# One wait more in each turn: GpSimd's subtraction behind VectorE's max of the same turn

## The chip, the cores and the metric

The kernel runs on one core of a Trainium2 chip. The metric is the device time of one execution in microseconds (us). The engines are TensorE (PE; its weight loads are shown apart as PEld), VectorE (DVE), ScalarE (ACT), GpSimd (POOL) and SyncE (SP), which only issues transfers here. All five run on their own and meet by semaphores. [...]

## The reference, cut to what matters

Two layers work on eight images x of 256 channels and 32 x 32 places. The change lies in the first, an attention with a learned position bias. For each image and each of four heads, 1024 queries look at 64 sampled keys. The bias of a query and a key is a small network of two inputs, the signed logarithms of the distances in x and in y:

```python
bias = jnp.sign(pos) * jnp.log1p(jnp.abs(pos))
bias = jax.nn.relu(bias @ cpb_w1.T + cpb_b1)      # first layer, 64 hidden channels
bias = jax.nn.relu(bias @ cpb_w2.T + cpb_b2)      # second layer, 64 x 64
bias = bias @ cpb_w3.T + cpb_b3                   # third layer, one value
attn = jax.nn.softmax(sim + bias, axis=-1)
```

It is computed for every pair of query and key: 8 x 4 x 1024 x 64 pairs. The second layer of the kernel is a sigmoid attention over the 1024 tokens of an image, followed by a mixture of eight experts of which each token takes two.

## The kernel before, in words

**Steps and turns.** The bias network is cut into steps. One step holds 128 partitions (two keys times 64 hidden channels) by 1024 elements (two heads, 16 rows and 32 columns of queries). An image has 128 steps (STEPS), taken two at a time in 64 turns (TURNS), so the main loop has 8 x 64 = 512 turns. The step with the even number n and the one with the odd number go different ways.

**First layer.** The network's first layer separates into a term of the column (`ta`) and a negated term of the row (`nb`), prepared once for 16 steps by `terms` (its `scale` is L439 on ScalarE and L440 on VectorE, its `second` is L446 on TensorE and L451 on ScalarE). An even step is a subtraction ta - nb on GpSimd (L465), followed by a ReLU in place on ScalarE (`rectify`, L470). An odd step is a single max(ta, nb) on VectorE (L463), which differs from the ReLU of the difference by nb; that term is put back later through `nc_`. Both read two SBUF tensors and write one `h1` tile of 128 x 1024, of which there are six buffers.

**Second layer.** `second_layer` runs four groups of matmuls on TensorE (L478) for each step into a PSUM tile `h2p`, of which there are two: one for the even and one for the odd step of a turn. The even one is emptied by ScalarE with a ReLU (L484), the odd one by VectorE with a max against `nc_` (L486). So the second layer of one turn needs L484 and L486 of the turn before.

**Third layer and the rest.** `third_layer` adds the product with the third weights into the PSUM tile `sim` (L505) every other turn. Beside this chain, each turn carries a piece of other work, paced by generators: the preparation of the next image (`prep`: the powers L260, the depthwise convolution L286, the sampling weights L368), `softmax` (L537), the sigmoid attention (`attention`: matmuls L713 and L727, sigmoid L718, normalising L579, L580 and L587, the residual sum L680, scatters L775) and the experts with their sums (`experts` L921, L926, L939 and L947; `combine` L984 and the gathers L992).

**Order.** In turn n the loop calls, in this order: the first layer of turn n + 2 (`first_layer`, even and then odd), the second layer of turn n, the ReLU of the new even step, the third layer where it is due, and the other work. `in_order` fixes each engine's queue in the order in which the code issues. On VectorE this gives max of n + 2, L486 of n, other work of n; on ScalarE L484 of n, L470 of n + 2, other work of n; on GpSimd the subtraction of n + 2 and then other work of n. Between engines only semaphores count, so GpSimd may run ahead of VectorE as far as the six buffers let it.

Of the kernel before, what the change touches and what calls it, by code (L numbers as in the profile page):

```python
# [9 lines left out]
F32 = mybir.dt.float32  # L10
I32 = mybir.dt.int32
AF = mybir.ActivationFunctionType
ALU = mybir.AluOpType
# [3 lines left out]
P = 128  # L17
# [53 lines left out]
def second_form(b, table, n):  # L71

    return n % 2 == 1
# [30 lines left out]
def tile_conv_attn_hybrid(ctx: ExitStack, tc: tile.TileContext, x, par, qw, w1, w2_, cst, out):  # L104
    nc = tc.nc
# [7 lines left out]
    hpool = ctx.enter_context(tc.tile_pool(name="h", bufs=1))  # L113
# [9 lines left out]
    def big(name):  # L123
        return t8.tile([P, 2, N], F32, tag="t8", name=name)
# [19 lines left out]
    def xin(b):  # L144
        return x[b].rearrange("(k p) h w -> p k (h w)", p=P)
# [278 lines left out]
    def terms(b, k, h, part):  # L424
        number = 4 * k + 2 * h + part
        fd = sts[b]["fd"].rearrange("k (s r) f -> k r s f", r=2)
        ta = abpool.tile([P, 16, 2, 32], F32, name="ta")
        nb = abpool.tile([P, 16, 2, 16], F32, name="nb")
        nc_ = abpool.tile([P, 2, 8, 16], F32, name="nc")
        taf = ta.rearrange("p s g x -> p s (g x)")  # L430
        nbf = nb.rearrange("p s g y -> p s (g y)")
        ss = slice(part * 16, (part + 1) * 16)
        for r in range(2):
            rs = slice(64 * r, 64 * r + 64)
            nc.sync.dma_start(out=taf[rs], in_=fd[k, r, ss, 0:64].partition_broadcast(64))
            nc.sync.dma_start(out=nbf[rs], in_=fd[k, r, ss, 64 + 32 * h : 96 + 32 * h].partition_broadcast(64))

        def scale():
            nc.scalar.activation(taf, taf, AF.Identity, bias=par_("cb1"), scale=par_("w1x"))  # L439
            nc.vector.tensor_scalar(nbf, nbf, par_("w1y"), -1.0, ALU.mult, ALU.mult)  # L440

        def second():
            cps = [psum("cp") for _ in range(2)]
            for r, g in ((0, 0), (1, 1), (0, 1), (1, 0)):
                rs, gs = slice(64 * r, 64 * r + 64), slice(64 * g, 64 * g + 64)
                nc.tensor.matmul(  # L446
                    cps[r][gs, 0:128], lhsT=par_("w2")[rs, gs], rhs=nb[rs, 1::2, g, :],
                    start=True, stop=True, tile_position=(64 * r, 64 * g),
                )
            for r in range(2):  # L450
                nc.scalar.activation(  # L451
                    nc_[:, r].rearrange("p s y -> p (s y)"), cps[r][:, 0:128], AF.Identity, bias=ncb2,
                )

        return (ta, nb, nc_, b, number), scale, second

    def first_layer(terms_, n):
        ta, nb, nc_, of, number = terms_
        h1 = hpool.tile([P, 2, 16, W], F32, name="h1", bufs=6)
        a = ta[:, n].unsqueeze(2).to_broadcast([P, 2, 16, W])  # L460
        b = nb[:, n].unsqueeze(3).to_broadcast([P, 2, 16, W])
        if second_form(of, number, n):
            nc.vector.tensor_tensor(h1, a, b, ALU.max)  # L463
            return h1, nc_[:, :, n // 2]
        nc.gpsimd.tensor_tensor(h1, a, b, ALU.subtract)  # L465
        return h1, None

    def rectify(h1, nc_):
        if nc_ is None:
            nc.scalar.activation(h1, h1, AF.Relu)  # L470
# [3 lines left out]
    def second_layer(h1, nc_):  # L474
        h2p = ps_h.tile([P, 2, 512], F32, tag="h2p", name="h2p")
        for r, g in ((0, 0), (1, 1), (0, 1), (1, 0)):
            rs, gs = slice(64 * r, 64 * r + 64), slice(64 * g, 64 * g + 64)
            nc.tensor.matmul(  # L478
                h2p[gs, r, :], lhsT=par_("w2")[rs, gs], rhs=h1[rs, g].rearrange("p y x -> p (y x)"),
                start=True, stop=True, tile_position=(64 * r, 64 * g),  # L480
            )
        h2 = hpool.tile([P, 2, 512], F32, name="h2", bufs=6)
        if nc_ is None:
            nc.scalar.activation(h2, h2p, AF.Relu, bias=par_("cb2"))  # L484
            return h2
        nc.vector.tensor_tensor(  # L486
            h2.rearrange("p r (y x) -> p r y x", x=W), h2p.rearrange("p r (y x) -> p r y x", x=W),
            nc_.unsqueeze(3).to_broadcast([P, 2, 16, W]), ALU.max,
        )
        return h2  # L490
# [507 lines left out]
    class Side:  # L998
# [5 lines left out]
        def step(self):  # L1004
            busy = False
            if self.waiting and not (sorting and self.busy):
                busy = self.busy
                self.busy = next(self.waiting[0], None)
                if self.busy is None:
                    self.waiting.pop(0)  # L1010
                    self.busy = True
            if self.left and not busy and not sorting:
                self.left = next(self.prep, self) is not self
# [10 lines left out]
    table, scale, second = terms(0, 0, 0, 0)  # L1024
    while "sampled" not in sts[0]:
        next(first)
    scale()
    second()
    h1s = [first_layer(table, n) for n in range(4)]
    for h in h1s:  # L1030
        rectify(*h)
    run(first)
# [4 lines left out]
    def place(t):  # L1037
        b, s = divmod(t, STEPS)
        return b, s // 64, s // 32 % 2

    def logits(t):
        b, k, h = place(t)
        ss = third_layer(sts[b], k, h, t // 4 % 8, h2s[:4])
        del h2s[:4]
        if ss is None:
            return None
        if (k, h) == (0, 0):
            os_[b] = big("o")
        if (k, h) == (1, 1):
            sts[b]["last"] = ss  # L1050
        else:
            return softmax(sts[b], k, h, ss, os_[b], aside)

    def residual(b):
        xres[b] = big("x")
        nc.sync.dma_start(out=xres[b], in_=xin(b))

    def advance(what):
        for steps in list(what):
            if next(steps[1], what) is what:  # L1060
                what.remove(steps)
# [3 lines left out]
    def mix(b, i):  # L1065
        of = mixtures[0][0] if mixtures else NB
        if of == b - 2 and b < NB - 1:
            due = i in (24, 26) or i > 26 and i % 2 and i not in (35, 37, 39, 59, 61, 63)
        elif of == b - 3:
            due = i == 9  # L1070
        else:
            due = b == NB - 1 and (i >= TURNS - 2 if of == b - 1 else of < b and i > 9 and (i % 2 or i % 3 == 0))
        if due:
            step(mixtures)
# [5 lines left out]
    for n in range(NB * TURNS):  # L1080
        b, i = divmod(n, TURNS)
        if i == 0:
            steps = iter(())
            if b + 1 < NB:
                xb = big("xb")
                nc.sync.dma_start(out=xb, in_=xin(b + 1))
                steps = prep(b + 1, xb, sts[b + 1])
            side = Side(steps)
        if b == 0 and i in (8, 16):
            nc.sync.dma_start(  # L1090
                out=xss[i // 8 - 1].rearrange("(t p) c -> p t c", p=P),
                in_=zero.unsqueeze(1).to_broadcast([P, ROWS // P, C]),
            )
        if i == 46:
            residual(b)
        coming_ = (n // 8 + 1) * 16
        if coming_ < total and n % 8 == 0:
            b_, k_, h_ = place(coming_)
            coming, scale, second = terms(b_, k_, h_, coming_ // 16 % 2)
        if n % 8 == 6 and coming_ < total:  # L1100
            table = coming
        new = []
        if n + 2 < NB * TURNS:
            new = [first_layer(table, (2 * n + 4 + r) % 16) for r in range(2)]
        h1s += new
        h2s += [second_layer(*h1s.pop(0)) for _ in range(2)]
        for h in new:
            rectify(*h)
        ready = n % 2 == 0 and n and logits(2 * n - 1)
        if coming_ < total:  # L1110
            if n % 8 == 3:
                scale()
            elif n % 8 == 4:
                second()
        if i > 4:
            side.step()
        if ready:
            side.waiting.append(ready)
        if i == 0 and b:
            mains.append((b, below))  # L1120
        elif i == 53:
            above, below = attention(b, sts[b], os_.pop(b), {})
            mains.append((b, above))
        advance(mains)
        mix(b, i)
        step(sums)
        if i == TURNS - 1:
            side.finish()
    logits(total - 1)
    mains.append((b, below))  # L1130
    n = sorted_ = 0
# [119 lines left out]
```

## Time and profile before

| What | us |
|---|---|
| median of 3 runs | 3145.4 (3139.6 to 3148.86) |
| profiled execution | 3125.55 |
| its span, first to last instruction | 3123.8 |
| TensorE busy | 2832.1 (91%) |
| VectorE busy | 2170.5 (69%) |
| ScalarE busy | 1824.4 (58%) |
| GpSimd busy | 1558.2 (50%) |

The granted TensorE clock was 0.975 on average. A busy share is an average over stages: the first 200 us hold the start-up, where TensorE is busy for 131 us, and the last 274 us, after the 512 turns, hold the last image's attention and experts, where it is busy for 218 us. In a line of the profile, "L465 POOL" is line 465 of the kernel on GpSimd; the tiles follow as output<-inputs, then partitions x elements. In a line of waits come the total in us, the number of times and the longest.

### The profile page before, as it was taken

What the parts mean: (1) busy time and instruction counts of PE and PEld (TensorE: products, weight loads), DVE (VectorE), ACT (ScalarE), POOL (GpSimd) and SP (SyncE); (2) the same over time, 40 slices, a digit from 0 to 9 for tenths busy, and PEclk for the clock granted to TensorE, in tenths of its full rate; (3) what the DMA queues carried; (4) which work ended last, traced back from release to release, by engine and by line L of the source; (5) the groups of instructions that cost most, each with busy time, mean ns of one, the idle gap of its engine ahead of it and who ended that gap; (6) DMA issues with size and microseconds to landing.
All of it is one profiled execution on the core that took longest, in us unless ns stands there. A gap on an engine that the chain in (4) does not pass through costs nothing. (4 is left out here: it accounts for less than half of the span.)

```text
span 3123.8 us, 51635 instructions
## 1 busy us (share of the span) xinstructions
PE 2832.1 (91%) x19592; PEld 1395.6 (45%) x19592; DVE 2170.5 (69%) x2999; ACT 1824.4 (58%) x2533; POOL 1558.2 (50%) x945
## 2 busy tenths in 40 slices
PE   3888998899999999999999999899999999979975
PEld 2223343233545344453545445354444545514764
DVE  4897678967776687857876678766877574595122
ACT  3666565665576566665566656665666666554322
POOL 2546454744455364645556455553646443383122
PEclk7999999999999999999999999999999999989998
DMA  3312101211256125531346223561245325631386
GB/s 106 83 32 48 21 14 32 58 38 21 75 139 187 23 63 140 168 107 43 77 111 208 51 57 100 144 179 33 61 132 173 88 78 153 173 97 57 112 280 221
DMA packets 428297, 311.21 MB, mean 100 GB/s; under 512 B 284432, under 2 KB 368656, under 8 KB 428048
## 3 DMA queue, kind: packets, MB, share of 16 engines
q1 hardware_dynamic: 415472, 273.14, 32.7%
q0 software_dynamic: 12288, 33.57, 3.4%
q8 instruction: 154, 2.52, 0.3%
q10 hardware_dynamic: 288, 1.20, 0.1%
q14 instruction: 95, 0.78, 0.1%
HBM read 239.93 MB, written 67.90 MB: 99 GB/s over the span
## 5 line engine op out<-in xcount | busy, mean ns | idle before, releaser
L465 POOL TENSOR_TENSOR h<-ta,nb 128x1024 f32<-128x1024 f32 x512 | 1071.6, 2095 | 1036.2 <-PE h2p L478 913.1
L478 PE MATMUL h2p<-h,pr__100 64*64 64x512 f32 x8192 | 1028.3, 610 | 131.8 <-DVE h L486 107.5
L486 DVE TENSOR_TENSOR h<-h2p,nc 128x1024 f32<-128x1024 f32 x512 | 624.6, 1220 | 461.4 <-PE h2p L478 454.7
L484 ACT ACTIVATE h<-h2p,pr__100 128x1024 f32<-128x1024 f32 x512 | 570.9, 1115 | 517.0 <-PE h2p L478 515.8
L463 DVE TENSOR_TENSOR h<-ta,nb 128x1024 f32<-128x1024 f32 x512 | 769.2, 1503 | 0.3
L470 ACT ACTIVATE h<-h 128x1024 f32<-128x1024 f32 x512 | 538.0, 1051 | 63.4 <-POOL h L465 63.2
L478 PEld LDWEIGHTS h2p<-h,pr__100 64*64 64x64 f32 x8192 | 253.7, 133 | 658.0 <-issue 295.1
L505 PE MATMUL sim<-h,pr__100 128*32 128x512 f32 x4096 | 511.5, 618 | 0.0
L505 PEld LDWEIGHTS sim<-h,pr__100 128*32 128x32 f32 x4096 | 109.5, 112 | 377.8 <-issue 377.8
L713 PE MATMUL ap<-qt,tn 128*128 128x256 f32 x1024 | 250.5, 388 | 0.5 <-ACT nc L451 0.5
L727 PE MATMUL vp<-tt,sg 128*128 128x256 f32 x1024 | 243.3, 381 | 0.3 <-ACT sg L718 0.3
L992 POOL DMA_INDIRECT gs<-ys,slot x128 | 139.0, 1086 | 175.3 <-DMA ys<-yt 55.7
L713 PEld LDWEIGHTS ap<-qt,tn 128*128 128x128 f32 x1024 | 185.2, 190 | 88.5 <-issue 55.0
L947 ACT ACTIVATE ht<-hp,w 128x128 f32<-128x128 f32 (+1 forms) x366 | 108.6, 377 | 196.8 <-PE hp L939 173.2
L921 PE MATMUL yp<-w,ht 128*128 128x256 f32 x792 | 196.2, 390 | 13.7 <-DMA w<-in_w 7.0
L727 PEld LDWEIGHTS vp<-tt,sg 128*128 128x128 f32 x1024 | 193.2, 190 | 33.2 <-issue 6.9
L939 PE MATMUL hp<-xg,w 128*128 128x128 f32 (+1 forms) x1464 | 197.0, 287 | 6.7 <-ACT gk L307 2.8
L939 PEld LDWEIGHTS hp<-xg,w 128*128 128x128 f32 x1464 | 187.8, 194 | 18.3 <-ACT gk L307 3.7
L775 POOL DMA_INDIRECT xs<-ut,slot x128 | 167.8, 1311 | 51.0 <-DVE slot L869 29.4
L921 PEld LDWEIGHTS yp<-w,ht 128*128 128x128 f32 x792 | 144.4, 191 | 73.0 <-issue 34.0
L926 DVE TENSOR_TENSOR yt<-yp,w 128x512 f32<-128x512 f32 x99 | 68.3, 690 | 153.5 <-PE yp L921 127.3
L286 DVE SCALAR_TENSOR_TENSOR oc<-qp,pr__100,oc 128x128 f32<-128x128 f32 x280 | 168.9, 603 | 7.2
(266 smaller groups left out, 2468.0 us busy)
## 6 DMA issues: line engine op xcount, KB each, us to landing
w<-in_w SPq DMA_DIRECT2D x183, 384.0 KB, 3.6
w<-in_w SPq DMA_DIRECT2D x183, 257.0 KB, 3.7
ta<-fd SPq DMA_DIRECT2D x128, 256.0 KB, 5.5
xl<-xs SPq DMA_DIRECT2D x99, 256.0 KB, 3.7
ys<-yt SPq DMA_DIRECT2D x99, 256.0 KB, 2.3
nb<-fd SPq DMA_DIRECT2D x128, 128.0 KB, 5.3
xb<-in_x SPq DMA_DIRECT2D x8, 1024.0 KB, 7.2
x<-in_x SPq DMA_DIRECT2D x8, 1024.0 KB
```

What stands on the lines that cost most here:

```text
L286: nc.vector.scalar_tensor_tensor(oc, tap, dw[:, t : t + 1], oc, ALU.mult, ALU.add)
L463: nc.vector.tensor_tensor(h1, a, b, ALU.max)
L465: nc.gpsimd.tensor_tensor(h1, a, b, ALU.subtract)
L470: nc.scalar.activation(h1, h1, AF.Relu)
L478: nc.tensor.matmul(h2p[gs, r, :], lhsT=par_("w2")[rs, gs], rhs=h1[rs, g].rearrange("p y x -> p (y x)"), start=True, stop=True, tile_positi ...
L484: nc.scalar.activation(h2, h2p, AF.Relu, bias=par_("cb2"))
L486: nc.vector.tensor_tensor(h2.rearrange("p r (y x) -> p r y x", x=W), h2p.rearrange("p r (y x) -> p r y x", x=W), nc_.unsqueeze(3).to_broad ...
L505: nc.tensor.matmul(sim[32 * q : 32 * q + 32, :], lhsT=par_("z3")[:, 15 - m : 47 - m], rhs=h2s[2 * u + q // 2][:, q % 2, :], start=False, s ...
L713: nc.tensor.matmul(ap[:, u, :], lhsT=tn[:, k, m0 : m0 + P], rhs=qt[:, k, quarter(q)], start=(k == 0), stop=(k == 1),)
L727: nc.tensor.matmul(vp[:, i, :], lhsT=sg_[:, u, i * P : (i + 1) * P], rhs=tt[:, 2 * mp + u, :], start=(first and u == 0 and i == 0), stop=( ...
L921: nc.tensor.matmul(yp[:, s, :], lhsT=ht[:, f, s * P : (s + 1) * P], rhs=f2[:, s * several // 2, f * C : (f + 1) * C], start=(f == 0), stop ...
L939: nc.tensor.matmul(hp[:, f, us], lhsT=f1[:, u, k * C + f * P : k * C + (f + 1) * P], rhs=xg[:, k, us], start=(k == 0), stop=(k == 1),)
```

## The change

A new function `first_layers` takes both steps of a turn. It takes the two `h1` buffers first, then issues the odd step's max and after it the even step's subtraction, and adds a dependency, carried by a semaphore, of the subtraction on the max. `first_layer` is given its buffer and returns its instruction as a third value. The four steps ahead of the loop are made by two calls. The values computed are the same.

```diff
-    def first_layer(terms_, n):
+    def first_layers(terms_, n):
+        h1s = [hpool.tile([P, 2, 16, W], F32, name="h1", bufs=6) for _ in range(2)]
+        out = [first_layer(terms_, n + r, h1s[r]) for r in (1, 0)]
+        tc.add_manual_dep(
+            out[1][2].ins, out[0][2].ins.name,
+            mybir.DependencyInfo(mybir.DependencyClass.Sync, mybir.DependencyReason.DATA),
+            reason="a port in turns",
+        )
+        return [h[:2] for h in reversed(out)]
+
+    def first_layer(terms_, n, h1):
         ta, nb, nc_, of, number = terms_
-        h1 = hpool.tile([P, 2, 16, W], F32, name="h1", bufs=6)
         a = ta[:, n].unsqueeze(2).to_broadcast([P, 2, 16, W])
         b = nb[:, n].unsqueeze(3).to_broadcast([P, 2, 16, W])
         if second_form(of, number, n):
-            nc.vector.tensor_tensor(h1, a, b, ALU.max)
-            return h1, nc_[:, :, n // 2]
-        nc.gpsimd.tensor_tensor(h1, a, b, ALU.subtract)
-        return h1, None
+            return h1, nc_[:, :, n // 2], nc.vector.tensor_tensor(h1, a, b, ALU.max)
+        return h1, None, nc.gpsimd.tensor_tensor(h1, a, b, ALU.subtract)
...
-    h1s = [first_layer(table, n) for n in range(4)]
+    h1s = [h for n in (0, 2) for h in first_layers(table, n)]
...
         if n + 2 < NB * TURNS:
-            new = [first_layer(table, (2 * n + 4 + r) % 16) for r in range(2)]
+            new = first_layers(table, (2 * n + 4) % 16)
```

## The prediction

> **What bounds the kernel now.** I read the page's busy shares first, then its table of slices, then the costliest groups, the list of waits by engine, and last the timeline of single turns.
>
> ```profile
> PE 2832.1 (91%) x19592; PEld 1395.6 (45%) x19592; DVE 2170.5 (69%) x2999; ACT 1824.4 (58%) x2533; POOL 1558.2 (50%) x945
> PE   3888998899999999999999999899999999979975
> ```
>
> TensorE (PE) is busy for 91% of the span, nine tenths or more in most slices of the loop. The stretches 200 to 1000, 1000 to 2000 and 2000 to 2850 us hold 738, 947 and 797 us of PE work in 2650 us, so 167 us of idle TensorE is all that a better order can win inside the loop. A turn takes 5.45 us on average (the mean distance of the maxes). The change touches no matmul; it acts through what TensorE waits for.
>
> ```profile
> L465 POOL TENSOR_TENSOR h<-ta,nb 128x1024 f32<-128x1024 f32 x512 | 1071.6, 2095 | 1036.2 <-PE h2p L478 913.1
> L486 DVE TENSOR_TENSOR h<-h2p,nc 128x1024 f32<-128x1024 f32 x512 | 624.6, 1220 | 461.4 <-PE h2p L478 454.7
> L463 DVE TENSOR_TENSOR h<-ta,nb 128x1024 f32<-128x1024 f32 x512 | 769.2, 1503 | 0.3
> L470 ACT ACTIVATE h<-h 128x1024 f32<-128x1024 f32 x512 | 538.0, 1051 | 63.4 <-POOL h L465 63.2
> ```
>
> After the bar come busy us and mean ns, then the idle time before. The max (L463) has a mean of 1503 ns but a median of 1218 ns: 512 x 0.285 = 146 us too much. The subtraction (L465) has 2095 against a median of 1916 ns: 92 us. L486, which has one SBUF input, shows no such spread (1220 mean, 1224 median).
>
> ```profile
> PE h2p L478 <- DVE h L486: 107.5, 85, 5.5
> PE h2p L478 <- ACT h L484: 22.7, 40, 3.7
> ```
>
> Of the idle time of TensorE, 107.5 us is for VectorE to empty the second-layer bank of an odd step (L486), 22.7 us for ScalarE to empty that of an even step (L484). A VectorE that is late is today's leading fault, and a slow max stands directly ahead of L486 on its queue.
>
> ```profile
> 1014.44 1.22 DVE L463 TENSOR_TENSOR h<-ta,nb 128x1024 f32<-128x1024 f32 x1
> 1015.06 2.37 POOL L465 TENSOR_TENSOR h<-ta,nb 128x1024 f32<-128x1024 f32 x1 [0.98 <-PE h2p L478]
> 1015.81 1.22 DVE L486 TENSOR_TENSOR h<-h2p,nc 128x1024 f32<-128x1024 f32 x1
> 1016.95 1.57 DVE L463 TENSOR_TENSOR h<-ta,nb 128x1024 f32<-128x1024 f32 x1
> ```
>
> The subtraction that starts inside a max ends 1.77 us after the max does; the next max, started before that subtraction's end at 1017.43, ends 1.09 us after it. Each held the other up. L486, between them, was not touched.
>
> [...] 32 times ScalarE stood for the subtraction, 63.2 us.
>
> **The change, part by part.** No instruction is added or removed, and each of the five engines has its instructions in the same order as before, SyncE's transfers included. What changes is that each of the 512 subtractions waits for the max of its own turn. The buffers of the two swap roles in the rotation of six; that asks of the max only a ReLU of three turns ago, long done: nothing, and a late ReLU of that age would already hold TensorE.
>
> *Gain.* Subtraction and max of one turn cannot meet, nor can a subtraction run ahead into the maxes of earlier turns. Excess of the mean over the median, or over the shortest where half are disturbed (L440): L463 146 us, L286 (603-446) x 280 = 44, L440 (1094-475) x 64 = 40, L984 (661-477) x 128 = 24; with the smaller lines about 320 us on VectorE. To price it I took from the timeline, turn by turn, how late L486 starts after the last matmul of its tile (0.07 us is the quickest): 349 us in 496 turns. In 267 us of that, VectorE had worked without a break since some excess, so the lateness goes with it. Where TensorE idled for that L486, the idle time that goes is 87 us of 101. Not all the excess will go: a subtraction now starts as its max ends and runs 1.92 us, L486 covers 1.22 at least, and the next two-input operation can be blocked for up to 0.7. I take three quarters: **65 us gained**.
>
> *Loss.* Behind the waiting subtraction on GpSimd's queue stand powers (L579, L260), scaling (L368), scatters (L775), gathers (L992) and residual sums (L680); on average they move by 1.8 to 2.7 us, L680 by 4.8, and their users come one to three turns later, so I take nothing, with 20 us if VectorE meets a late gather at L984 (14.4 us today). The price is at ScalarE. There the order is L484(k), ReLU L470(k+2), the turn's other work, L484(k+1). Today the subtraction runs ahead: 469 of 512 start before their own max, in the median 4.3 us before, and end 3.4 us before their ReLU starts. Bound to the max they start 5.9 us later (median, max's end minus today's start). With the maxes where they are, 343 of 490 ReLUs would find their input missing, 862 us in all; with the maxes earlier by the VectorE excess ahead of them, 464 us, nearly 1 us a turn. ScalarE stands for that time, then follow 1.05 us of ReLU and the work behind it: sigmoid L718, GELU L947, normalising L587, bank copies L451, and L484(k+1).
>
> How much reaches TensorE? L484 has in the median 3.2 us until the matmul that needs its bank, L486 only 2.0. I followed each delay down ScalarE's queue (each instruction at its own duration) and set it against the start of the matmul that waits for it. For L484 alone 39 us stick out (97 with the maxes as they are); for all of ScalarE's results, the longest of each turn, 108 us (237). A held TensorE is held once: the max of turn k hangs on L486 of turn k-3, so a delay buys the next two turns the same time. Counting the running delay as the larger of the turn before's and this turn's stick-out plus that of three turns ago, 81 us remain with all excess gone, 149 with none, 88 with three quarters. A TensorE that comes earlier for its gain meets the same late ReLU and gives part of it back: between nothing and a half (33 us); I take 12. **About 100 us lost.**
>
> *Sum.* +100 - 65 = +35 us against the profiled execution of 3125.6 us (span 3123.8 and 1.8 around it): 3160. The median of the runs shown, 3145.4, is 19.8 us above that execution, so 3180.
>
> **The rivals.**
> *Faster: the port was the fault.* All 87 us go, perhaps the 107.5 whole, and only L484's 39 us is paid, because ScalarE's other results are needed a turn later and have room that my turn-by-turn count is too strict on. For it: L486 has the smallest slack and the longest wait; ScalarE is 42% idle. Against it: in-order ScalarE stands for the ReLU, whatever its idle share. -87 + 39 = -48, with the whole wait -68: 3077 to 3097 as a median. It decides once less than 65 us of ScalarE's delay reaches TensorE.
> *They cancel.* Two equal exchanges of a wait on L486 for one on L484: within 0.3% (9 us, about what a measurement of this kernel can tell from no change).
> *Much slower.* The excess stays because the late subtraction meets the side work of VectorE (L286, L984) instead, and maxes come no earlier: 149 to 237 us lost and little won, 3295 to 3380.
> *Nothing changes.* It would need a subtraction whose wait is implied already; in the built program all 512 wait for a max, none did before. Left out.
>
> **How the numbers follow.** Slower (my forecast, with the much slower end) 0.50, faster 0.42, cancelled 0.08: loss and gain are each near 90 us, each from a first-order count that leaves out how one delay moves the next, so the sign is only leaning. The likeliest case alone spans 3155 to 3240. The range takes in the faster rival down to its end and a little beyond, and most of the losing side: 3070 to 3260.
>
> **What would show it.** Right: L463's mean near 1.25 us; the wait of TensorE for L486 below 40 us; L470's wait for L465 up from 63 to 400 or more; L484's wait at TensorE up from 23 to 60 or more, with ScalarE named ahead of side matmuls. L465 named as waiting for L463. Wrong on the gain: L463 still above 1.4 us. Wrong on the loss: L470's wait large while TensorE's idle time in the loop falls under 130 us; then the faster rival holds.

## The result: slower by 1.3%, and where the time stands in the profile after

The changed kernel takes 3186.15 us (median of 4 runs, 3181.38 to 3187.09) against 3144.8 us before (4 runs): a ratio of 1.0129, with a 95% interval of 1.0111 to 1.0148. The forecast was 3180 us, with 0.50 on slower. The profiled execution took 3187.09 us, its span is 3185.3 us; that of the kernel before, 3125.55 us, was some 20 us quicker than its median, so that the two pages lie further apart than the medians. Line numbers above 463 have moved: L465 is now L475 (the subtraction), L463 L474 (the max), L470 L479 (the ReLU), L484 L493 and L486 L495 (the two that empty the second layer's banks), L478 L487 (the second layer's matmuls). "The port" stands in what follows for what the prediction read from the timeline between a max and a subtraction. Counted over the whole trace before, the 274 maxes that overlap a subtraction took 1.75 us in the mean, the 238 others 1.22; the 271 subtractions that overlap a max took 2.25 us, the 241 others 1.92. Of the 142 maxes that start inside a subtraction, 138 end after it, by 1.08 us in the median. L486 took 1.22 us with a subtraction beside it and without. L440, L286 and L984 were longer with one as well: 1.12, 1.08 and 1.56 us in the mean, against 0.48, 0.47 and 0.51. What in the chip brings this about is not shown.

The page after, engines, slices and the four groups that answer to those before:

```profile
PE 2846.9 (89%) x19592; PEld 1412.5 (44%) x19592; DVE 2024.3 (64%) x2999; ACT 1836.3 (58%) x2533; POOL 1417.4 (44%) x945
PE   4888999899999999999989999999999999988976
...
L475 POOL TENSOR_TENSOR h<-ta,nb 128x1024 f32<-128x1024 f32 x512 | 984.5, 1923 | 1400.8 <-DVE h L474 963.4
...
L495 DVE TENSOR_TENSOR h<-h2p,nc 128x1024 f32<-128x1024 f32 x512 | 625.2, 1221 | 613.6 <-PE h2p L487 608.8
L479 ACT ACTIVATE h<-h 128x1024 f32<-128x1024 f32 x512 | 541.5, 1058 | 526.6 <-POOL h L475 524.2
...
L474 DVE TENSOR_TENSOR h<-ta,nb 128x1024 f32<-128x1024 f32 x512 | 678.7, 1326 | 0.4
```

VectorE has 146 us less to do and GpSimd 141 us less: the subtraction is back at its undisturbed length (1923 ns; 1924 in the mean before where no max overlapped), the max has come down from 1503 to 1326 ns. Less is lost at the port (74 of the 512 maxes overlap a subtraction, 274 before), and the kernel is slower. ScalarE's ReLU (L479) points to the reason: it now stands 524 us for the subtraction, where it stood 63 us.

The waits of the kernel after (total us, times, longest):

```profile
POOL h L475 <- DVE h L474: 963.4, 331, 10.7
ACT h L479 <- POOL h L475: 524.2, 303, 4.4
PE h2p L487 <- ACT h L493: 98.0, 92, 3.7
PE h2p L487 <- DVE h L495: 14.8, 27, 0.8
```

In the second layer TensorE's wait for VectorE has gone (107.5 to 14.8 us), and its wait for ScalarE has grown (22.7 to 98.0 us). These two together are less than before, 113 us against 130, so they do not account for the loss. The rest stands in the other matmuls: over all of them TensorE waits 236 us for ScalarE (101 before) and 51 us for VectorE (161 before). Two lines of that rest, which were 1.1 and 3.3 us before:

```profile
PE bp L648 <- ACT tt L596: 12.3, 24, 2.5
PE ov L571 <- ACT nc L451: 11.2, 7, 1.6
```

L596 (the normalising, L587 before) and the bank copy L451 are work of ScalarE that stands on its queue behind the waiting ReLU. In this trace it ran nothing else in the meantime: 510 of its 512 L493 are followed directly by an L479, as 510 of the 512 L484 were by an L470 before, and the two that are not belong to the last two turns, which have no new step. One turn of the timeline after shows the chain in the order of time:

```profile
1026.35 1.22 DVE L474 TENSOR_TENSOR h<-ta,nb 128x1024 f32<-128x1024 f32 x1
1026.80 1.11 ACT L493 ACTIVATE h<-h2p,pr__100 128x1024 f32<-128x1024 f32 x1 [1.67 <-PE h2p L487]
...
1027.71 1.91 POOL L475 TENSOR_TENSOR h<-ta,nb 128x1024 f32<-128x1024 f32 x1 [3.76 <-DVE h L474]
...
1029.65 1.06 ACT L479 ACTIVATE h<-h 128x1024 f32<-128x1024 f32 x1 [1.75 <-POOL h L475]
```

The subtraction starts 0.14 us after its max ends and ends at 1029.62; ScalarE had been free since 1027.91 and stood for 1.75 us, with the turn's other work behind the ReLU. Taken over turns 6 to 500, a subtraction starts 1.36 us after its max starts (median; 4.3 us ahead of it before) and ends 0.03 us before its ReLU starts (3.4 us before). Between turn 4 and turn 500 the stretch grew from 2725.5 to 2772.2 us and the idle time of TensorE in it from 183 to 220 us. The other 10 us are TensorE at work: it was busy for 2542.4 us there before and for 2552.2 us after.

### The profile page after: what moved, and what is told of

It is laid out like the page before. It is cut to its first block, busy times and chain, and to the rows that moved or that the text cites. A ratio compares the mean times of both kernels' runs of the same rounds, so it can differ in the third digit from the quotient of the medians.

```text
span 3185.3 us, 51557 instructions
## 1 busy us (share of the span) xinstructions
PE 2846.9 (89%) x19592; PEld 1412.5 (44%) x19592; DVE 2024.3 (64%) x2999; ACT 1836.3 (58%) x2533; POOL 1417.4 (44%) x945
## 5 line engine op out<-in xcount | busy, mean ns | idle before, releaser
L475 POOL TENSOR_TENSOR h<-ta,nb 128x1024 f32<-128x1024 f32 x512 | 984.5, 1923 | 1400.8 <-DVE h L474 963.4
L487 PE MATMUL h2p<-h,pr__100 64*64 64x512 f32 x8192 | 1028.4, 615 | 119.1 <-ACT h L493 98.0
L495 DVE TENSOR_TENSOR h<-h2p,nc 128x1024 f32<-128x1024 f32 x512 | 625.2, 1221 | 613.6 <-PE h2p L487 608.8
L479 ACT ACTIVATE h<-h 128x1024 f32<-128x1024 f32 x512 | 541.5, 1058 | 526.6 <-POOL h L475 524.2
L493 ACT ACTIVATE h<-h2p,pr__100 128x1024 f32<-128x1024 f32 x512 | 570.5, 1114 | 309.0 <-PE h2p L487 308.8
L474 DVE TENSOR_TENSOR h<-ta,nb 128x1024 f32<-128x1024 f32 x512 | 678.7, 1326 | 0.4
L487 PEld LDWEIGHTS h2p<-h,pr__100 64*64 64x64 f32 x8192 | 259.8, 134 | 640.4 <-issue 302.7
L514 PE MATMUL sim<-h,pr__100 128*32 128x512 f32 x4096 | 499.4, 606 | 0.0
L1001 POOL DMA_INDIRECT gs<-ys,slot x128 | 132.0, 1031 | 154.3 <-DVE xc L993 26.7
L784 POOL DMA_INDIRECT xs<-ut,slot x128 | 140.8, 1100 | 49.0 <-DVE slot L878 25.9
L286 DVE SCALAR_TENSOR_TENSOR oc<-qp,pr__100,oc 128x128 f32<-128x128 f32 x280 | 157.5, 562 | 7.2
```

What stands on the lines that cost most here:

```text
L286: nc.vector.scalar_tensor_tensor(oc, tap, dw[:, t : t + 1], oc, ALU.mult, ALU.add)
L474: return h1, nc_[:, :, n // 2], nc.vector.tensor_tensor(h1, a, b, ALU.max)
L475: return h1, None, nc.gpsimd.tensor_tensor(h1, a, b, ALU.subtract)
L487: nc.tensor.matmul(h2p[gs, r, :], lhsT=par_("w2")[rs, gs], rhs=h1[rs, g].rearrange("p y x -> p (y x)"), start=True, stop=True, tile_positi ...
L495: nc.vector.tensor_tensor(h2.rearrange("p r (y x) -> p r y x", x=W), h2p.rearrange("p r (y x) -> p r y x", x=W), nc_.unsqueeze(3).to_broad ...
L514: nc.tensor.matmul(sim[32 * q : 32 * q + 32, :], lhsT=par_("z3")[:, 15 - m : 47 - m], rhs=h2s[2 * u + q // 2][:, q % 2, :], start=False, s ...
```

## The experiments

Each ratio is to the kernel before, run on the same chip. Differences between runs are given as differences of ratios, times 3145 us; from the two intervals each carries some 8 us either way, and more where more than two runs enter. The theory: ScalarE, which ran its work in the order of issue in both traces (510 of 512 turns, above), stands for a subtraction that is bound to a late max. The rivals: new meetings at the port, GpSimd's own queue, or any tie between the two engines.

**e1: the change without the wait.**

```diff
         out = [first_layer(terms_, n + r, h1s[r]) for r in (1, 0)]
-        tc.add_manual_dep(
-            out[1][2].ins, out[0][2].ins.name,
...
-        )
         return [h[:2] for h in reversed(out)]
```

> The change without its added wait: max issued ahead of the subtraction and both buffers taken first, no dependency between the two. ReLU theory (the loss comes from ScalarE standing in its queue for a subtraction that is bound to a late max): the subtraction runs ahead again, though about 1 us later than before because its buffer is now the one that an odd step leaves; ratio to before 0.998 to 1.005, ReLU's wait for the subtraction under 150 us (524 with the wait). Rival, order and buffers: the swapped buffers alone carry the loss; ratio 1.010 or more.

Ratio 0.9859 (0.9839 to 0.9878), 3087.25 us: neither side's number. ScalarE's wait for the subtraction is 75 us, as the theory had it. What remains of the change without the wait is a change by itself, and a good one. On top of it the wait costs 1.0129 - 0.9859 = 0.0270, 85 us, and something else in the change gives 44 us as long as there is no wait.

**e5 and e6: what that something is.** The change issues the max first, and because of that the buffers of even and odd steps change places at every round of the six. e5 keeps the order of issue of the change and gives each parity three buffers of its own; e6 keeps the order of before and exchanges the buffers.

```diff
# e5, against the changed kernel
-        h1s = [hpool.tile([P, 2, 16, W], F32, name="h1", bufs=6) for _ in range(2)]
+        h1s = [hpool.tile([P, 2, 16, W], F32, name=f"h1{r}", bufs=3) for r in range(2)]
         out = [first_layer(terms_, n + r, h1s[r]) for r in (1, 0)]
-        tc.add_manual_dep(
...
# e6, against the changed kernel
+    taken = [0]
...
-        h1s = [hpool.tile([P, 2, 16, W], F32, name="h1", bufs=6) for _ in range(2)]
-        out = [first_layer(terms_, n + r, h1s[r]) for r in (1, 0)]
-        tc.add_manual_dep(
...
+        swap = (taken[0] // 3) % 2
+        taken[0] += 1
+        h1s = [hpool.tile([P, 2, 16, W], F32, name=f"h1{r ^ swap}", bufs=3) for r in range(2)]
+        out = [first_layer(terms_, n + r, h1s[r]) for r in (0, 1)]
+        return [h[:2] for h in out]
```

> No wait; the max is issued ahead of the subtraction, but even and odd steps keep three buffers each, as before. Buffer theory (the gain of the run without the wait comes from the subtraction taking the buffer of an odd step, so that it starts about 0.8 us later, after the whole second layer of three turns ago): ratio to before 0.996 to 1.004. Rival, issue order: ratio 0.982 to 0.990, as without the wait.

> No wait; the subtraction is issued first, as before, but even and odd steps exchange their three buffers every third turn, so that the subtraction takes an odd step's buffer. Buffer theory: it starts 0.1 us after the second layer of three turns ago ends (0.7 us ahead of that before); ratio 0.982 to 0.990. Rival, issue order: 0.996 to 1.004.

e5: 0.9993 (0.9982 to 1.0005). e6: 0.9854 (0.9831 to 0.9878). The buffers carry all of the 44 us. In the timeline the subtraction starts 0.68 us before the second layer of three turns ago has ended in the median before, because an even step's buffer is free half way through; with an odd step's buffer it starts 0.12 us after that end. The sum of what VectorE's maxes lose at the port is much the same (146 us before, 155 in e6), so it is not that they lose less there. They seem to meet elsewhere: counted from the timeline, about 265 us of the time by which L486 is late can be put down to such a loss in the unbroken stretch of VectorE work ahead of it in the kernel before (187 turns), and about 150 us in e6 (some 115 turns), with the median taken as an instruction's undisturbed length. TensorE's wait for that instruction goes down with it (107.5 us before; in e6 L486 are the matmuls and L494 is the max that was L486):

```profile
PE h2p L486 <- DVE h L494: 86.3, 81, 3.8
```

That the exchange of buffers is the cause is shown by e5 and e6. That it works through where the meetings fall is read from these counts, and no run sets it alone.

**e2, e3 and e7: the ReLU a turn later.** The ReLU of a new even step is kept back and issued in the next turn, behind that turn's L484.

```diff
-        for h in new:
+        for h in late:
             rectify(*h)
+        late = new
```

`late` starts as an empty list ahead of the loop. e2 is the changed kernel with it, e3 the kernel before, e7 the run without the wait (e1).

> The changed kernel, with the ReLU of an even step issued one turn later on ScalarE (still a turn ahead of the matmuls that read it). ReLU theory: ScalarE no longer stands for the subtraction (wait under 60 us) while the gain on VectorE stays; ratio to before 0.970 to 0.990. Rival, GpSimd's queue (powers, scatters and gathers behind the waiting subtraction carry the loss): ratio stays 1.008 to 1.016.

> The kernel before with the same later ReLU and no wait: the control. ReLU theory: there is little to win, ReLU waits for the subtraction for only 63 us there; ratio 0.992 to 1.003. Rival, the later ReLU is a better order for ScalarE by itself: ratio as low as that of the run with wait and late ReLU, which then proves nothing about the wait.

> The run without the wait, with the ReLU a turn later: the control for the run with wait and late ReLU (0.981). If the wait wins at the port once the ReLU no longer stands: ratio 0.987 to 0.996 here, that is 0.6% or more above that run. Rival, the port is worth nothing on this path: ratio 0.978 to 0.984, the same as with the wait.

e2: 0.9811 (0.9795 to 0.9828), from 1.0129: 100 us. e3: 1.0047 (1.0031 to 1.0063), a little above what was expected. e7: 0.9848 (0.9825 to 0.9870), against 0.9859 without the later ReLU. The later ReLU by itself wins nothing or loses; only where the wait is, it gives 100 us back. So these 100 us hang on ScalarE standing for the subtraction. e7 lies between its two ranges, 0.0037 above e2: 12 us, with 9 either way. With the ReLU out of the way the wait wins something over the run without it, but little. The ReLU's group in e2:

```profile
L479 ACT ACTIVATE h<-h 128x1024 f32<-128x1024 f32 x512 | 538.3, 1051 | 34.8 <-POOL h L475 34.4
```

The price of the later ReLU is seen in another line of e2, the matmuls, which now wait for a ReLU that comes just ahead of them:

```profile
L487 PE MATMUL h2p<-h,pr__100 64*64 64x512 f32 x8192 | 1014.2, 605 | 137.3 <-ACT h L479 102.2
```

GpSimd's queue is as late in e2 as in the changed kernel (the subtraction starts 1.36 us after its max in both), and 100 us are back: that rival falls.

**e9 and e10: the wait where there is nothing to win at the port.** The subtraction is replaced by two fills, which read nothing, so that the first layer of the even steps is left out; in e10 the first fill waits for the max.

```diff
...
-        return h1, None, nc.gpsimd.tensor_tensor(h1, a, b, ALU.subtract)
+        filled = [nc.gpsimd.memset(h1, 0.25) for _ in range(2)]
+        return h1, None, filled[0]
```

> The run without the wait, with the subtraction replaced by two fills of the same tile (a constant, nothing read from SBUF, about 1.8 us together): the bias network of the even steps is left out. It prices the port with no wait. If the port is what the fills avoid: the max's mean falls from 1.51 to 1.24 us or less, and the ratio to before from 0.986 to between 0.960 and 0.975. Rival, the port costs nothing on the path: 0.983 to 0.989. If fills meet the max at the port as well, its mean stays above 1.4 us and the run prices nothing.

> The same fills, the first of which waits for the max of its turn: the wait alone, with nothing to win at the port. The even steps' first layer is left out here too. ReLU theory: 80 to 130 us above the fills without the wait (0.025 to 0.041 in ratio), ScalarE waits for the fills for 400 us or more. Rival, the loss of the changed kernel comes from new meetings at the port: within 0.5% of the fills without the wait.

e9: 0.9610 (0.9594 to 0.9626). The page of e9 has the max at its undisturbed length (1221 ns, against 1510 in e1) beside a GpSimd that is nearly as busy (two fills of 956 ns for a subtraction of 2072 ns in e1). So these fills, which read nothing and write the same kind of tile, did not hold the max up. The 1.8 us expected for two of them can be estimated from the fill L182 of the kernel before: 2139 ns for 2448 elements, so 0.89 us for 1024.

```profile
L470 POOL MEMSET h<- 128x1024 f32 x1024 | 978.9, 956 | 1085.9 <-PE h2p L483 886.7
...
L469 DVE TENSOR_TENSOR h<-ta,nb 128x1024 f32<-128x1024 f32 x512 | 625.2, 1221 | 0.3
```

Without a wait the port costs 0.9859 - 0.9610 = 0.0249, 78 us. e10: 1.0032 (1.0016 to 1.0048). The wait alone costs 0.0422, just above the range expected, or 133 us, where fills and max do not hold each other up (954 and 1219 ns, as against 956 and 1221 in e9): the rival of new meetings falls too. The waits of e10 are those of the changed kernel again (L480 the ReLU, L494 the even bank):

```profile
ACT h L480 <- POOL h L475: 438.6, 277, 4.5
PE h2p L488 <- ACT h L494: 95.5, 92, 3.7
```

The 133 us are a price and the 85 us of the real wait a net, so that the wait should win 48 us of the port's 78 and lose 133. The 48 us are a difference of four ratios, with 11 us either way, and hold as far as fills stand for the subtraction; e2 and e7, with the later ReLU, show only 12.

**e4: the wait turned round.** The subtraction is issued first and the max waits for it.

```diff
-        out = [first_layer(terms_, n + r, h1s[r]) for r in (1, 0)]
+        out = [first_layer(terms_, n + r, h1s[r]) for r in (0, 1)]
...
-        return [h[:2] for h in reversed(out)]
+        return [h[:2] for h in out]
```

> The wait turned round: the subtraction is issued first and VectorE's max waits for it. ReLU theory: the subtraction is early again and ScalarE does not stand (under 100 us), VectorE stands in its queue instead of at the port, so the lateness of the second layer's max is as before: ratio 0.998 to 1.008. Rival, any tie between the two engines costs the same: ratio 1.010 to 1.016.

1.0145 (1.0127 to 1.0163). The number is that of the rival, but not its reason. ScalarE does not stand (63.7 us, as before); VectorE does:

```profile
DVE h L474 <- POOL h L475: 142.0, 70, 7.5
...
PE h2p L487 <- DVE h L495: 157.0, 108, 5.5
```

A max now stands behind a subtraction that is late itself, up to 7.5 us. The time by which L486 is late rises from 353 to 463 us. The expectation took the wait at a semaphore to be no worse than the loss at the port; by these 110 us it was. The control is another one, too: with the subtraction issued first the buffers keep their places (it starts 0.68 us ahead of the end of the second layer of three turns ago, as before), so this wait costs 46 us over its own control, and that of the change 85 us over e1.

**e8: the same tie, one turn back.** The subtraction waits for the max of the turn before its own.

```diff
-        tc.add_manual_dep(
-            out[1][2].ins, out[0][2].ins.name,
...
+        if maxes:
+            tc.add_manual_dep(
+                out[1][2].ins, maxes[-1],
...
+        maxes.append(out[0][2].ins.name)
```

> The subtraction waits for the max of the turn before its own: the same tie, one turn less late. ReLU theory: ScalarE waits for the subtraction under 120 us, ratio 0.978 to 0.990 (the run without the wait has 0.986). Rival, any tie of GpSimd to VectorE costs: ratio 1.00 or more.

0.9764 (0.9743 to 0.9786), 3060.8 us: a tie need not cost. ScalarE waits 95.9 us for the subtraction, the subtraction is at 1952 ns, and only 155 pairs of a subtraction and a max overlap (282 without the wait). It beats e1 by 0.0095, 30 us. The rival, that any tie of GpSimd to VectorE costs, falls with it.

**e11 and e12: the ReLU at the end of the turn.** In place of a whole turn later, the ReLU is issued behind the turn's other work; e11 is the changed kernel with it, e12 is e8 with it.

```diff
-        for h in new:
-            rectify(*h)
         ready = n % 2 == 0 and n and logits(2 * n - 1)
...
         step(sums)
+        for h in new:
+            rectify(*h)
```

> The changed kernel, with the ReLU issued at the end of the same turn, behind the turn's other work on ScalarE instead of ahead of it. ReLU theory: the other work no longer stands for the subtraction, ScalarE's wait for it falls under 250 us, and the matmuls have the ReLU half a turn earlier than in the run with the ReLU a whole turn later (0.981); ratio 0.970 to 0.985. Rival, the second layer's ReLU of the next turn is what stands: it is still behind, ratio 1.000 to 1.013.

> The wait for the max of one turn back (0.976), with the ReLU at the end of the turn. ReLU theory: there 96 us of ScalarE's wait for the subtraction are left to win, most of it not on the path: ratio 0.965 to 0.977. Rival, the later ReLU holds up the matmuls instead: 0.978 to 0.990.

e11: 0.9743 (0.9727 to 0.9759), 121 us below the changed kernel with the same wait on GpSimd. e12: 0.9701 (0.9684 to 0.9717), 3054.32 us, the fastest version that computes the whole network and 3% ahead of the kernel before. In e11 the ReLU still stands for 243 us, but with less behind it:

```profile
L479 ACT ACTIVATE h<-h 128x1024 f32<-128x1024 f32 x512 | 542.6, 1060 | 244.5 <-POOL h L475 243.2
```

The ReLU at the end of the turn was not run without a wait. So it stays open how much of the gain of e11 over the kernel before is the wait's, and how much would come from the ReLU's new place and from the buffers alone.

**Idle and busy TensorE.** A difference between two profiled executions has two parts: TensorE idles longer, or its 19592 matmuls take longer. The first lines of the pages of e2, e9 and e10, in this order (spans 3068.2, 3019.1 and 3157.0 us):

```profile
PE 2794.9 (91%) x19592; PEld 1393.3 (45%) x19592; DVE 2041.8 (67%) x2999; ACT 1830.7 (60%) x2533; POOL 1418.5 (46%) x945
PE 2799.6 (93%) x19592; PEld 1394.5 (46%) x19592; DVE 1911.8 (63%) x2999; ACT 1822.2 (60%) x2533; POOL 1427.2 (47%) x1457
PE 2834.9 (90%) x19592; PEld 1411.8 (45%) x19592; DVE 1889.7 (60%) x2999; ACT 1837.1 (58%) x2533; POOL 1391.3 (44%) x1457
```

From e9 to e10 the span grows by 138 us: TensorE idles 103 us longer, and the same matmuls are busy 35 us longer. From the changed kernel to e2 it shrinks by 117 us, 65 idle and 52 busy. From the kernel before to the changed one it grows by 62 us, 47 idle and 15 busy. The second part goes with the granted TensorE clock: 0.975 before, 0.969 in the changed kernel, 0.986 in e2, 0.982 in e9 and 0.972 in e10; busy time times clock is the same in the five within 0.5%. The whole time shows it too: on the chip of e9, one execution of the kernel before took 3140.3 us at a clock of 0.974, another 3153.5 us at 0.969. Why the versions differ in clock is not shown. Idle time alone does not order them: e3 idles 322 us at 0.978, the kernel before 292 us at 0.975. So the 100 us of e2 and the 133 us of e10 are prices of the whole effect, of which TensorE's waits are the larger part (65 of 117 us and 103 of 138 by the pages) and the longer matmuls at the lower clock a smaller one.

## Why the prediction was right, and which of its terms were not

- *Sign, sum and mechanism.* Forecast +35 us on the profiled execution, 3180 us as a median; measured 3186. The mechanism is the one forecast: ScalarE, its work in the order of issue, stands for the late subtraction (524 us). e2 and e10 show it, with e3, e7 and e9 as their controls; e11 fits.
- *The signs named.* L470's wait "400 or more": 524 us, between the 464 and 862 us counted with the maxes earlier and as they were. TensorE's wait for L486 "below 40": 14.8 us. L484's wait "60 or more": 98 us. ScalarE is named ahead of side matmuls, and L465 (now L475) as waiting for the max. These held. L463's mean "near 1.25" did not: 1.326 us, so 56 of 146 us remain, 62% gone where three quarters were taken.
- *Loss, forecast 100 us.* It measured 133 us (e10). The count was one of TensorE's idle time, and in idle time the pages of e9 and e10 have 103 us, close to it. What it lacked is that the same matmuls would also take longer, 35 us by these pages; no term stood for that.
- *Gain, forecast 65 us.* What the change wins beside that price is 133 less 41, 92 us, some 9 us either way; in idle time by the pages it is 103 less 47, 56 us. The whole port is worth 78 us without the wait (e9), on top of the buffers. Of the 87 us counted in TensorE's idle time the pages have 72 us gone from the kernel before to e9, buffers and port together.
- *A step that was passed over: the buffers.* "The buffers of the two swap roles ... nothing." The step asked only what the max must wait for in its new buffer. The subtraction's side was not asked: it must now wait for the odd step's matmuls. Without the wait that is worth 44 us, on the good side (e1, e6). Whether it is worth anything with the wait is not shown: there the subtraction starts 4.9 us after these matmuls in the median, so that the wait delays it by far more than the buffer does, and the wait with the buffers of before was not run. The 92 us may be 44 of the buffers and 48 of the port, or the port's alone.
- *Luck.* In device time the loss was 33 us too small and the gain 27 us too small, and the two errors took each other's place: +133 - 92 = +41 us, against +100 - 65 = +35. The 92 us come from this sum and don't test it.
- *The faster rival* was right about VectorE and wrong about ScalarE. It needed less than 65 us of ScalarE's delay to reach TensorE, because only L484 would count; 103 us of idle time did (e10), and TensorE's longer wait for ScalarE stands in the other matmuls as well as behind L484. With the ReLU out of the way the same wait stands in kernels that are 1.9% (e2) and 2.6% (e11) faster than before, but only 12 us of e2's gain is shown to be the wait's.
- *Nothing for GpSimd's other work* is not contradicted: in e2 and e11 GpSimd is as late as in the changed kernel, and both are faster than before.

## What to carry to other kernels

Before an engine is made to wait, look at the queue of the engine that reads its result: here a ReLU at the head of ScalarE's queue stood for 524 us and held up what was issued behind it, on an engine that was idle for 42% of the time; the wait alone cost 133 us (e10). If the wait is wanted, move the reader back in its own queue (e11, 2.6% faster than before), tie the wait to an instruction that is a turn older (e8, 2.4%), or do both (e12, 3.0%). And when issue order changes which buffer an instruction is given, price the other instruction's new wait as well, and measure the change without the wait: here that alone was 1.4% faster.

## What was not expected of the hardware

The time that two instructions lose at the port did not price it. The maxes lost 146 us before and 155 us with the buffers exchanged, and the kernel took 1.46% less time in the second case. That it matters where they meet is the likely reading; no run sets that alone, and part of the gain goes with a higher granted clock (TensorE busy for 2814.1 us at 0.980 in e6, for 2832.1 us at 0.975 before).

The granted clock of a single core moved with the version of the kernel: the same 19592 matmuls were busy for 2794.9 us at 0.986 (e2) and for 2854.2 us at 0.968 (e4). What sets it stays open.
